# A fused attention and mixture-of-experts block: the slot's order rewritten with the projection in front, LayerNorms as a two-tensor operation, the last two weight centrings moved to VectorE

## The chip, the cores and the metric

The program runs on one NeuronCore of a Trainium2 chip. The core has TensorE (PE: matrix products and transposes into PSUM), VectorE (DVE), ScalarE (ACT) and GpSimd (POOL), each with its own instruction queue that is worked off strictly in order; SyncE (SP) issues transfers. The metric is the device time of one execution in microseconds, smaller is better. The kernel before took 807.15 us, the median of three runs (806.92 to 808.42).

## The reference

A sandwich block on x of shape 8 x 256 x 256 (batch, sequence, width), all float32. Attention has 16 query heads and 4 key/value heads of width 128; the expert layer has 8 experts of 176 hidden units, 2 for each token, and a shared expert of 352.

```
def layernorm(x): return (x - mean(x)) / sqrt(var(x) + 1e-5)          # over the last axis

# attention, on xn = layernorm(x)
q, k, v = split(xn @ w_qkv.T)                     # 16, 4 and 4 heads of 128
q = rope(layernorm(q) * qn_g + qn_b)              # rope(z) = z * cos + rotate_half(z) * sin
k = rope(layernorm(k) * kn_g + kn_b)
w = softmax(mask(q @ k.T / sqrt(128)))            # causal
x = x + layernorm((w @ v) @ w_o.T)

# experts, on xf = layernorm(x)
weights, indices = top_k(softmax(xf @ gate_w.T), 2); weights /= weights.sum()
out = sum over the chosen experts e of weights_e * ((silu(xf @ w_gate[e]) * (xf @ w_up[e])) @ w_down[e])
out += sigmoid(xf @ shgate_w) * ((silu(xf @ shw_gate) * (xf @ shw_up)) @ shw_down)
x = x + layernorm(out)
```

The mean of a head is taken out of the weights instead of the projected rows ("centring": the mean over the 128 columns of a head is subtracted from w_qkv), so that a head's LayerNorm needs only the mean of its squares.

## The kernel before

The kernel has two halves. The first runs attention for all eight batches and routes the tokens; the second runs the experts block by block. The change is in the first half, but for the LayerNorm helper, which both use.

**The slot loop.** After some hand-written steps at the start, the first half is one loop over slots s (L850). In each slot, functions issue one step each of several pipelines, and the order in which they stand in the loop body is the order on every engine's queue (`manual_schedule`: nothing is reordered). Twelve slots make a batch; there are 12 projections and 12 attention units in a batch. In slot s the loop works on projection j = s and on unit u = s - 7:

- `multiply(j)`, L384: the projection, four passes of 128x512 on PE into a PSUM tile `qkv`. Projection j is one group of 512 columns for one half of the sequence: k, k, v, v, then four pairs of q.
- `square`, L402, on ACT; `deviation`, L408, the sum of squares on DVE; `power`, L417, the reciprocal root on POOL. For v, `square` is only a copy (L399), and there is no LayerNorm or rope.
- `normalise`, L426: ACT scales the four heads from PSUM into `qn`.
- `rope_cos`, L440, on DVE and `rope_sin`, L452, two instructions on POOL, both read `qn`; `rope_offset`, L465, POOL, adds the table of offsets; `rope_sum`, L481, DVE, adds the two.
- `turn_heads`, L496: four transposes on PE into PSUM tile `tq`, and the copy to SBUF, L497, on ACT.
- `score`, L508 and L518 (PE); `maximum`, L528 (DVE); `exponential`, L539 (ACT); `inverse`, L547 (DVE); `weights`, on POOL (L554) for the units of four heads, every third unit, and on ACT (L559) for those of two; `turn_weights`, L570 (PE, PSUM tile `tp`); `copy_weights`, L575 (DVE); `value`, L588 (PE); `copy_value`, L599 (ACT); `output`, L607 (PE): the product with w_o of the batch before, 3, 3, 3, 3, 4, 0 steps in turn.

Some slots carry rarer steps. Counting slots within a batch as s mod 12: 0 and 6 have no output step and take the statistics of the finished attention rows (`residual`, then `residual_sum`); 1 and 7 those of the new residual (`inner`, `inner_rows`, which also writes the rows to memory by a transfer on SP's queue); 2 and 5 those of the next batch's x (`prepare`, `prepared`), transposed in 6 and 7 (`turn_x`). Slots 2 and 8 transpose the residual rows (`turn_inner`), 3 and 9 route (`route`, `gates`), 4 and 10 count and mark (`rank`, `mark`, `shares`), 5 and 11 enter the result (`enter`). All the row statistics have the same form: `norm_stats` (DVE L252, L253, L255; then POOL L256), `norm_apply` (DVE L261).

**Order within a slot.** normalise(j-1), rope_sum(j-2), turn_weights and copy_weights(u-2), copy_value(u-3), inverse and weights(u-1), score and maximum(u), rope_cos and rope_sin(j-1), then multiply(j), square(j), turn_heads(j-2), the statistics, `turn_x`, `turn_inner`, the routing, rope_offset(j-1), deviation(j) and power(j), the LayerNorms' second halves, exponential(u), output, value(u-2).

**Buffers.** PSUM has two tiles each for projections (`mm`), for transposes (`tr`, shared by tq, tp and the rarer ones) and for scores (`sc`), and one each for `av` and `o`.

**The start.** Of the six groups of w_qkv, group 4 is centred on DVE (`means`, `centre`), group 5 (v) not at all, and groups 0 to 3 have their means taken on DVE and the addition done in eight instructions each on ACT (`centre_on_act`, L242): groups 2 and 3 inside the loop, in slots 7 and 9. The x of batch 1 is prepared in slots 7 and 8 and transposed in 9 and 10 (`late_x`).

Of the kernel before, what the change touches and what calls it, by code (L numbers as in the profile page):

```python
# [19 lines left out]
P = 128  # L20
# [28 lines left out]
def block_kernel(  # L49
# [184 lines left out]
    def centre(heads, wm):  # L234
# [2 lines left out]
            in1=wm[:, :, None].to_broadcast([P, KC * REP, D]), op=ALU.add,  # L237
        )

    def centre_on_act(heads, wm):  # L240
        for i in range(KC * REP):
            nc.scalar.activation(  # L242
                heads[:, i, :], heads[:, i, :], AF.Identity, bias=wm[:, i : i + 1]
            )
# [13 lines left out]

    def norm_apply(dst, src, name):
        mean, rstd = stats.pop(name)  # L260
        nc.vector.tensor_scalar(dst, src, mean, rstd, ALU.subtract, ALU.mult)  # L261

    ps_mm = ctx.enter_context(tc.tile_pool(name="ps_mm", bufs=2, space=PSUM))
    ps_tr = ctx.enter_context(tc.tile_pool(name="ps_tr", bufs=2, space=PSUM))
# [73 lines left out]
    with ExitStack() as actx:  # L338
# [74 lines left out]
        def power(b, j):  # L413
            if projections[b][j][0] == 5:
                return
            rstd = small.tile([P, REP], F32, tag="rstds", name=f"rstds_{b}_{j}")
            nc.gpsimd.tensor_tensor(rstd, now.pop(("ve", b, j)), nhalf, ALU.pow)  # L417
            now["rstd", b, j] = rstd

        def normalise(b, j):  # L420
            if projections[b][j][0] == 5:
                return
            ps, rstd = now.pop(("mm", b, j)), now.pop(("rstd", b, j))
            qn = rw.tile([P, REP, D], F32, tag="qn", name=f"qn_{b}_{j}", bufs=2)
            for h in range(REP):
                nc.scalar.activation(  # L426
                    qn[:, h, :], ps[:, h, :], AF.Copy, scale=rstd[:, h : h + 1]
                )
            now["qn", b, j] = qn
# [53 lines left out]
        def turn_heads(b, j):  # L483
            g, t = projections[b][j]
            if g == 5:
                return
            if t == 0:
                if g == 4:
                    seqs[b]["kT"] = akv.tile([P, HKV, S], F32, tag="kT", name=f"kT_{b}")
                else:  # L490
                    seqs[b]["qT"][g] = q4pool.tile([P, REP, S], F32, tag="q4", name="q4")
            dst = seqs[b]["kT"] if g == 4 else seqs[b]["qT"][g]
            tr = ps_tr.tile([P, REP, P], F32, tag="tr", name=f"tq_{b}_{j}")
            t1 = now.pop(("t1", b, j))
            for h in range(REP):
                nc.tensor.transpose(tr[:, h, :], t1[:, h, :], ident)  # L496
            nc.scalar.copy(dst[:, :, t * P : (t + 1) * P], tr)  # L497
# [268 lines left out]
                if i == place and 0 < b < B - 1:  # L766
                    f(b + 1, t)

        late_x = {7: ([prepare], [prepared]), 8: ([prepare], [prepared]), 9: ([turn_x], []), 10: ([turn_x], [])}
        FIRST = LAG  # L770
        means_at = {8: 3}
        centre_at = {7: 2, 9: 3}
        found = {}
        with tc.manual_schedule():

# [45 lines left out]
            rope_sin(0, 4)  # L821
            deviation(0, 2)
            power(0, 2)
            centre_on_act(*found.pop(1))
            rope_sum(0, 1)
            turn_heads(0, 1)
            rope_sum(0, 4)
            turn_heads(0, 4)
            multiply(0, 3)
            multiply(0, 6)  # L830
            normalise(0, 2)
            square(0, 3)
            square(0, 5)
            rope_cos(0, 2)
            rope_offset_early(0, 2)
            rope_sin(0, 2)
            deviation(0, 5)
            power(0, 5)
            found[2] = means(2)
            normalise(0, 5)  # L840
            square(0, 6)
            rope_sum(0, 2)
            turn_heads(0, 2)
            rope_cos(0, 5)
# [1 line left out]
            rope_sin(0, 5)  # L846
            deviation(0, 6)
            power(0, 6)
            LAST = B * NS + LAG + 3
            for s in range(FIRST, LAST):  # L850
                u, j = s - LAG, s
                each(normalise, j - 1)
                each(rope_sum, j - 2)
                each(turn_weights, u - 2)
                each(copy_weights, u - 2)
                each(copy_value, u - 3)
                each(inverse, u - 1)
                each(weights, u - 1)
                each(score, u)
                each(maximum, u)  # L860
                each(rope_cos, j - 1)
                each(rope_sin, j - 1)
                if s == FIRST:
                    each(rope_offset_early, j - 1)
                each(multiply, j)
                each(square, j)
                each(turn_heads, j - 2)
                if s == B * NS + 1:
                    parked[0, 0] = products(0, 0)
                elif s == B * NS + 8:  # L870
                    parked[0, 1] = products(0, 1, ps_o, "o")
                ends(s, [(residual, 5), (inner, 6)])
                begins(s, [(prepare, 0, 2), (prepare, 1, 5), (turn_x, 0, 6), (turn_x, 1, 7)])
                if s in late_x:
                    for f in late_x[s][0]:
                        f(1, s - FIRST if f is prepare else s - FIRST - 2)
                ends(
                    s,
                    [(turn_inner, 7), (route, 8), (gates, 8), (rank, 9), (mark, 9), (shares, 9), (enter, 10)],
                )  # L880
                if s > FIRST:
                    each(rope_offset, j - 1)
                each(deviation, j)
                if s in means_at:
                    found[means_at[s]] = means(means_at[s])
                if s in centre_at:
                    centre_on_act(*found.pop(centre_at[s]))
                each(power, j)
                ends(s, [(residual_sum, 5), (inner_rows, 6)])
                begins(s, [(prepared, 0, 2), (prepared, 1, 5)])  # L890
                if s in late_x:
                    for f in late_x[s][1]:
                        f(1, s - FIRST)
                each(exponential, u)
                for b, i in [divmod(s - OUT, NS)]:
                    if 0 <= b < B:
                        for o in range(OUTPUTS[i]):
                            output(b, sum(OUTPUTS[:i]) + o)
                each(value, u - 2)
                if s == B * NS:  # L900

                    wgu_sb = wpool.tile([P, KC, E * 2 * HE], F32, tag="w", name="wgu_sb")
                    for j, w in enumerate((wg, wu)):
                        for c in range(KC):
                            nc.sync.dma_start(
                                out=wgu_sb[:, c, :].rearrange("p (e g h) -> p e g h", g=2, h=HE)[
                                    :, :, j, :
                                ],
                                in_=w[c * P : (c + 1) * P, : E * HE].rearrange(
                                    "p (e h) -> p e h", h=HE  # L910
                                ),
                            )
# [389 lines left out]
```

## Time and profile before

| | |
|---|---|
| median of three runs | 807.15 us |
| the profiled execution: time, span | 801.91 us, 799.9 us |
| PE busy | 742.7 us, 93% of the span |
| DVE busy | 553.4 us, 69% |
| POOL busy | 488.0 us, 61% |
| ACT busy | 443.5 us, 55% |
| granted TensorE clock | 0.992 of full speed |
| transfers | 32.40 MB, most of it in the first 20 us and the last 100 us |

The profiled execution took 2.0 us outside its span, and was 5.2 us faster than the median of the runs. Busy shares are means over the whole span. The loop's first batch runs from about 35 to 102 us; from there to about 567 us PE is busy nearly all the time, in a pattern that repeats every batch; the experts follow. A start time of the next instruction of the same queue minus that of an instruction says what it costs; its own duration is longer, since instructions overlap at their ends. Of PE's matrix products, four passes make one product of the projection, since float32 takes two passes and there are two chunks of the width.

### The profile page before, as it was taken

What the parts mean: (1) busy time and instruction counts of PE and PEld (TensorE: products, weight loads), DVE (VectorE), ACT (ScalarE), POOL (GpSimd) and SP (SyncE); (2) the same over time, 40 slices, a digit from 0 to 9 for tenths busy, and PEclk for the clock granted to TensorE, in tenths of its full rate; (3) what the DMA queues carried; (4) which work ended last, traced back from release to release, by engine and by line L of the source; (5) the groups of instructions that cost most, each with busy time, mean ns of one, the idle gap of its engine ahead of it and who ended that gap; (6) DMA issues with size and microseconds to landing.
All of it is one profiled execution on the core that took longest, in us unless ns stands there. A gap on an engine that the chain in (4) does not pass through costs nothing.

```text
span 799.9 us, 11918 instructions
## 1 busy us (share of the span) xinstructions
PE 742.7 (93%) x3765; PEld 550.3 (69%) x3796; DVE 553.4 (69%) x1396; ACT 443.5 (55%) x1426; POOL 488.0 (61%) x526
## 2 busy tenths in 40 slices
PE   7588899999999999999999999999799989999994
PEld 4355577767776676767677766777588767777773
DVE  7776666788777777877887777668755645354556
ACT  3587677665747575766657475756542323333331
POOL 5678588386848675774878486657611253656423
PEclk9899999999999999999999999999999999999998
DMA  9300000000000000000000000000400333434322
GB/s 314 123 0 1 1 0 2 7 7 2 8 1 7 1 7 1 8 0 8 8 1 8 1 7 1 7 1 8 144 8 9 85 93 99 139 101 131 106 86 79
DMA packets 26917, 32.40 MB, mean 41 GB/s; under 512 B 2980, under 2 KB 23048, under 8 KB 26856
## 3 DMA queue, kind: packets, MB, share of 16 engines
q1 hardware_dynamic: 22896, 22.07, 8.5%
q0 software_dynamic: 3408, 9.31, 4.5%
q8 instruction: 31, 0.51, 0.3%
q10 hardware_dynamic: 552, 0.26, 0.1%
q14 instruction: 30, 0.25, 0.1%
HBM read 22.33 MB, written 9.31 MB: 40 GB/s over the span
## 4 chain that ended last, share of the span: by engine, by line
PE 59%; POOL 14%; DVE 13%; ACT 10%; issue 2%; DMA 1%; POOLq 0%; DVEq 0%
PE qkv L384 11%; PE o L607 8%; PE sc L508 7%; PE gu L1128 6%; PE av L588 6%; ACT qn L426 6%; POOL rstds L417 5%; PE gus L279 5%; POOL t L452 5%; PE py L1153 4%; PE tp L570 3%; POOL t L465 3%; PE tq L496 3%; PE sd L299 2%; DVE ves L408 2%
## 5 line engine op out<-in xcount | busy, mean ns | idle before, releaser
L384 PE MATMUL qkv<-w_qkv,xnT 128*128 128x512 f32 x384 | 182.7, 598 | 1.3 <-DVE xnT L374 1.2
L426 ACT ACTIVATE qn<-qkv,rstds 128x128 f32<-128x128 f32 x320 | 91.5, 370 | 151.3 <-POOL rstds L417 151.3
L452 POOL TENSOR_TENSOR t<-qn,sg_q 128x256 f32<-128x256 f32 x128 | 123.7, 986 | 49.8 <-ACT qn L426 49.8
L417 POOL TENSOR_TENSOR rstds<-ves,nhalf 128x4 f32<-128x4 f32 x80 | 87.7, 1096 | 96.4 <-DVE ves L408 96.2
L607 PE MATMUL o<-wo_sb,oT 128*128 128x256 f32 x512 | 125.1, 384 | 0.0
L508 PE MATMUL sc<-kT,q 128*128 128x128 f32 x768 | 108.7, 275 | 4.0 <-ACT q L497 2.3
L539 ACT ACTIVATE ex<-sc,nmx 128x128 f32<-128x128 f32 (+1 forms) x256 | 107.8, 455 | 2.7 <-DVE nmx L528 2.4
L588 PE MATMUL av<-pT,v 128*128 128x256 f32 (+1 forms) x320 | 100.4, 428 | 8.0 <-ACT oT L599 7.3
L508 PEld LDWEIGHTS sc<-kT,q 128*128 128x128 f32 x768 | 100.8, 191 | 5.0 <-ACT q L497 3.0
L384 PEld LDWEIGHTS qkv<-w_qkv,xnT 128*128 128x128 f32 x384 | 66.1, 192 | 52.5 <-issue 46.7
L607 PEld LDWEIGHTS o<-wo_sb,oT 128*128 128x128 f32 x512 | 91.5, 190 | 9.4
L481 DVE TENSOR_TENSOR t<-t,t 128x512 f32<-128x512 f32 x80 | 55.2, 692 | 49.2 <-POOL t L465 49.2
L496 PEld LDWEIGHTS tq<-ident,t 128*128 128x128 f32 x320 | 38.6, 143 | 66.4 <-issue 54.0
L465 POOL TENSOR_TENSOR t<-t,bb_q 128x512 f32<-128x512 f32 x61 | 77.6, 1272 | 2.7
L575 DVE COPY pT<-tp 128x512 f32<-128x512 f32 x96 | 65.6, 683 | 18.2 <-PE tp L570 18.1
L559 ACT ACTIVATE ex<-ex,rr 128x256 f32<-128x256 f32 x128 | 59.6, 527 | 28.1 <-DVE rr L547 28.1
L588 PEld LDWEIGHTS av<-pT,v 128*128 128x128 f32 x320 | 58.5, 190 | 20.2 <-ACT oT L599 10.5
L570 PEld LDWEIGHTS tp<-ident,ex 128*128 128x128 f32 x384 | 47.1, 141 | 31.5 <-ACT q L497 9.9
L496 PE MATMUL tq<-ident,t 128*128 128x128 f32 x320 | 49.4, 279 | 20.3 <-DVE t L481 20.3
L528 DVE TENSOR_REDUCE nmx<-sc 128x2 f32<-128x512 f32 (+1 forms) x96 | 64.2, 669 | 3.8 <-PE sc L508 3.4
L440 DVE TENSOR_TENSOR t<-qn,cg_q 128x512 f32<-128x512 f32 x64 | 47.5, 742 | 26.7 <-ACT qn L426 26.7
L408 DVE TENSOR_REDUCE ves<-sq 128x4 f32<-128x516 f32 x80 | 54.8, 685 | 14.2 <-ACT sq L402 14.2
(185 smaller groups left out, 1302.5 us busy)
## 6 DMA issues: line engine op xcount, KB each, us to landing
ys<-yb SPq DMA_DIRECT2D x39, 128.0 KB, 1.8
w_qkv<-in_wqkvT SPq DMA_DIRECT2D x6, 512.0 KB, 6.0
x_all<-in_x SPq DMA_DIRECT2D x8, 256.0 KB, 7.2
wo_sb<-in_woT SPq DMA_DIRECT2D x1, 2048.0 KB
xf_rows<-xf SPq DMA_DIRECT2D x16, 128.0 KB, 1.7
out<-yo SPq DMA_DIRECT2D x16, 128.0 KB, 1.7
wgu_sb<-in_wg SPq DMA_DIRECT2D x2, 704.0 KB, 5.3
wgu_sb<-in_wu SPq DMA_DIRECT2D x2, 704.0 KB, 8.4
```

The lines of the kernel that those rows point to most:

```text
L384: nc.tensor.matmul(ps.rearrange("p h d -> p (h d)"), lhsT=seqs[b]["xnT"][t][:, c, :], rhs=w_qkv[g][:, c, :], start=(c == 0), stop=(c == KC ...
L408: nc.vector.tensor_reduce(out=ve, in_=now.pop(("sq", b, j))[:, :, : D + 1], axis=AX.X, op=ALU.add)
L417: nc.gpsimd.tensor_tensor(rstd, now.pop(("ve", b, j)), nhalf, ALU.pow)
L426: nc.scalar.activation(qn[:, h, :], ps[:, h, :], AF.Copy, scale=rstd[:, h : h + 1])
L452: nc.gpsimd.tensor_tensor(t2[:, :, lo : lo + HD], qn[:, :, hi : hi + HD], sg[s][:, t : t + 1, lo : lo + HD].to_broadcast([P, REP, HD]), AL ...
L465: nc.gpsimd.tensor_tensor(t2, t2, bb[s][:, t : t + 1, :].to_broadcast([P, REP, D]), ALU.add)
L496: nc.tensor.transpose(tr[:, h, :], t1[:, h, :], ident)
L508: nc.tensor.matmul(sc[:, h, k * P : (k + 1) * P], lhsT=seqs[b]["qT"][g][:, r0 + h, t * P : (t + 1) * P], rhs=seqs[b]["kT"][:, g, k * P : ( ...
L539: nc.scalar.activation(ex[:, h, :], sc[:, h, :], AF.Exp, bias=nm[:, h : h + 1], accum_out=rs[:, h : h + 1],)
L570: nc.tensor.transpose(tr[:, c, :], ex[:, h, k * P : (k + 1) * P], ident)
L588: nc.tensor.matmul(now["av"][:, r0 : r0 + nh, :].rearrange("p h q -> p (h q)"), lhsT=seqs[b]["v"][:, k, g * D : (g + 1) * D], rhs=pT[:, k ...
L607: nc.tensor.matmul(now["o", b, t], lhsT=seqs[b]["oT"][h // REP, t][:, h % REP, :], rhs=wo_sb[:, h, :], start=(h == 0), stop=(h == H - 1),)
```

## The change

Five things change.

1. **The order within a slot.** `multiply(j)` goes to the front. Then follow normalise(j-1), rope_sum(j-2), inverse(u-1), copy_value(u-3), rope_cos(j-1), square(j), weights(u-1), rope_sin(j-1), turn_weights and copy_weights(u-2), deviation(j) and power(j), score and maximum(u), turn_heads(j-2), the statistics, rope_offset(j-1), the LayerNorms' second halves, exponential(u), output, `turn_x`, `turn_inner` and the routing, value(u-2). On POOL, power(j) and the statistics' powers so stand ahead of rope_offset(j-1); on DVE, copy_weights stands behind the cosine product, deviation between it and maximum, and the routing at the end of the slot.
2. **LayerNorms on rows.** `norm_apply` is a `scalar_tensor_tensor`, whose second tensor is the reciprocal root, repeated along the row, where it was a `tensor_scalar` with two scalars per partition.
3. **Centring.** Group 2 is centred on DVE ahead of the loop; group 3 on DVE in two halves, in slots 7 and 8 (`centre_chunk`). None is left to ACT inside the loop.
4. **The x of batch 1** is prepared in slots 9 and 10 and transposed in 11 and 12.
5. **The steps ahead of the loop** are put in another order: among others projection 6 ahead of projection 3, and square(5), deviation(5) and power(5) earlier.

```diff
+    def centre_chunk(g, c):
+
+        heads = w_qkv[g][:, c, :].rearrange("p (h d) -> p h d", d=D)
+        wm = small.tile([P, REP], F32, tag="wmc", name=f"wm_{g}_{c}")
+        nc.vector.tensor_reduce(out=wm, in_=heads, axis=AX.X, op=ALU.add)
+        nc.vector.tensor_scalar_mul(wm, wm, -1.0 / D)
+        nc.vector.tensor_tensor(
+            out=heads, in0=heads, in1=wm[:, :, None].to_broadcast([P, REP, D]), op=ALU.add
+        )
...
     def norm_apply(dst, src, name):
         mean, rstd = stats.pop(name)
-        nc.vector.tensor_scalar(dst, src, mean, rstd, ALU.subtract, ALU.mult)
+        nc.vector.scalar_tensor_tensor(
+            dst, src, mean, rstd.to_broadcast([P, HID]), ALU.subtract, ALU.mult
+        )
...
-        late_x = {7: ([prepare], [prepared]), 8: ([prepare], [prepared]), 9: ([turn_x], []), 10: ([turn_x], [])}
+        late_x = {9: ([prepare], [prepared]), 10: ([prepare], [prepared]), 11: ([turn_x], []), 12: ([turn_x], [])}
         FIRST = LAG
-        means_at = {8: 3}
-        centre_at = {7: 2, 9: 3}
         found = {}
...
             power(0, 2)
+            square(0, 5)
             centre_on_act(*found.pop(1))
             rope_sum(0, 1)
             turn_heads(0, 1)
             rope_sum(0, 4)
             turn_heads(0, 4)
+            normalise(0, 2)
+            multiply(0, 6)
             multiply(0, 3)
-            multiply(0, 6)
-            normalise(0, 2)
-            square(0, 3)
-            square(0, 5)
+            deviation(0, 5)
+            power(0, 5)
             rope_cos(0, 2)
             rope_offset_early(0, 2)
             rope_sin(0, 2)
-            deviation(0, 5)
-            power(0, 5)
-            found[2] = means(2)
             normalise(0, 5)
             square(0, 6)
+            square(0, 3)
             rope_sum(0, 2)
...
             power(0, 6)
+            centre(*means(2))
             LAST = B * NS + LAG + 3
             for s in range(FIRST, LAST):
                 u, j = s - LAG, s
+                each(multiply, j)
                 each(normalise, j - 1)
                 each(rope_sum, j - 2)
-                each(turn_weights, u - 2)
-                each(copy_weights, u - 2)
+                each(inverse, u - 1)
                 each(copy_value, u - 3)
-                each(inverse, u - 1)
+                each(rope_cos, j - 1)
+                each(square, j)
                 each(weights, u - 1)
-                each(score, u)
-                each(maximum, u)
-                each(rope_cos, j - 1)
                 each(rope_sin, j - 1)
                 if s == FIRST:
                     each(rope_offset_early, j - 1)
-                each(multiply, j)
-                each(square, j)
+                each(turn_weights, u - 2)
+                each(copy_weights, u - 2)
+                each(deviation, j)
+                each(power, j)
+                each(score, u)
+                each(maximum, u)
                 each(turn_heads, j - 2)
...
                 ends(s, [(residual, 5), (inner, 6)])
-                begins(s, [(prepare, 0, 2), (prepare, 1, 5), (turn_x, 0, 6), (turn_x, 1, 7)])
-                if s in late_x:
-                    for f in late_x[s][0]:
-                        f(1, s - FIRST if f is prepare else s - FIRST - 2)
-                ends(
-                    s,
-                    [(turn_inner, 7), (route, 8), (gates, 8), (rank, 9), (mark, 9), (shares, 9), (enter, 10)],
-                )
+                begins(s, [(prepare, 0, 2), (prepare, 1, 5)])
+                if s in late_x and prepare in late_x[s][0]:
+                    prepare(1, s - 9)
                 if s > FIRST:
                     each(rope_offset, j - 1)
-                each(deviation, j)
-                if s in means_at:
-                    found[means_at[s]] = means(means_at[s])
-                if s in centre_at:
-                    centre_on_act(*found.pop(centre_at[s]))
-                each(power, j)
                 ends(s, [(residual_sum, 5), (inner_rows, 6)])
                 begins(s, [(prepared, 0, 2), (prepared, 1, 5)])
                 if s in late_x:
                     for f in late_x[s][1]:
-                        f(1, s - FIRST)
+                        f(1, s - 9)
+                if s in (FIRST, FIRST + 1):
+                    centre_chunk(3, s - FIRST)
                 each(exponential, u)
                 for b, i in [divmod(s - OUT, NS)]:
                     if 0 <= b < B:
                         for o in range(OUTPUTS[i]):
                             output(b, sum(OUTPUTS[:i]) + o)
+                begins(s, [(turn_x, 0, 6), (turn_x, 1, 7)])
+                if s in late_x and turn_x in late_x[s][0]:
+                    turn_x(1, s - 11)
+                ends(s, [(turn_inner, 7), (route, 8), (gates, 8), (rank, 9), (mark, 9), (shares, 9), (enter, 10)])
                 each(value, u - 2)
```

## The prediction, made before the changed kernel was run

> **What bounds the kernel now.** I read the busy shares, then busy time by stretches, then the list of waits, then PE's and the side engines' timelines. Over one batch in the middle:
>
> ```profile
> 350.59:423.88 73.29, 70.99 (x374) 52.18 (x377) 57.26 (x140) 46.55 (x154) 50.93 (x53) 1.00 0.01 5
> ```
>
> (columns: stretch, length, then PE, weight loads, DVE, ACT, POOL; clock, DMA.) PE is at its limit, 70.99 of 73.29 us; no other engine is over 78%. The list of waits opens with an entry that looks like the thing to remove:
>
> ```profile
> ACT qn L426 <- POOL rstds L417: 151.3, 77, 3.6
> ```
>
> ACT waits 151 us for the power, but ACT has slack; it costs only what reaches PE. PE's timeline says how much that is:
>
> ```profile
> 345.50 0.63 PE L496 MATMUL tq<-ident,t 128*128 128x128 f32 x4 [0.95 <-DVE t L481]
> 353.44 1.12 PE L588 MATMUL av<-pT,v 128*128 128x512 f32 x2 [0.53 <-ACT oT L599]
> 390.25 0.65 PE L570 MATMUL tp<-ident,ex 128*128 128x128 f32 x4 [0.64 <-ACT q L497]
> ```
>
> A head transpose, a value product and a weight transpose wait once in a batch each. From start-to-start times (a transpose group costs 0.44, not its 0.60) the losses are 1.11, 0.69 and 0.81: 2.6 us a batch, about six batches, so 16 us is all that the steady part can give. The first batch (35.18 to 102.39 us, no outputs) loses more: 56.15 busy of 67.4 us.
>
> **What sets the pace beside PE** is the contention of DVE and POOL:
>
> ```profile
> 322.50 0.55 POOL L256 TENSOR_TENSOR rstd_f<-mv_f,nhalf 128x1 f32<-128x1 f32 x1
> 323.02 1.27 POOL L465 TENSOR_TENSOR t<-t,bb_q 128x512 f32<-128x512 f32 x1
> 323.09 1.36 DVE L261 TENSOR_SCALAR xf<-x_all,mv_f,rstd_f 128x256 f32<-128x256 f32 x1
> ```
>
> The row LayerNorm starts 0.07 us behind POOL's rope offset and ends 0.16 after it; alone it takes 0.41. A DVE operation with two SBUF tensors is held too:
>
> ```profile
> 575.96 0.72 POOL L622 TENSOR_TENSOR x_all<-x_all,y 128x256 f32<-128x256 f32 x1
> 576.03 1.19 DVE L481 TENSOR_TENSOR t<-t,t 128x512 f32<-128x512 f32 x1 [0.69 <-POOL t L465]
> ```
>
> That rope sum normally takes 0.69.
>
> **What the Trainium skill says.** "SBUF — State Buffer", section "SBUF: two separate sides": DVE and GpSimd share one port pair, held exclusively for a whole instruction by a GpSimd operation, by a DVE operation in a two-port mode, and, against a GpSimd operation that reads SBUF, by a DVE operation with two SBUF inputs. The lines above agree. "VectorE: DVE Perf Modes", section "The perf-mode tier table": float32 from SBUF, tensor_scalar runs at twice tensor_tensor's rate. Here the only scalar_tensor_tensor of 128x256 (L1174, L1178) takes 0.48 against 0.41.
>
> **The change, part by part.** A slot's work on PE is the same, in another cycle; its durations (start to start): projection 1.72, tp 0.44, scores 1.01, tq 0.44, 0.43 per output step, value 0.86, rarer steps 0.2 to 0.4. So a slot takes 4.5 to 4.7 without outputs (0 and 6), 5.8 to 6.1 with three, 6.65 with four.
>
> *Removed: the wait of normalise.* Power(j) now follows deviation(j) in mid-slot, before normalise(j) is due. So oT and q are copied in time, and their two waits (0.69, 0.81) lose that cause.
>
> *Added: a chain through the rope sum.* tq(j-2) needs rope_sum(j-2), which needs rope_offset(j-2); this now stands on POOL behind power(j-1) and the statistics' power of the slot before, and these wait for DVE's variance, maximum and statistics. On DVE the order is sum, reciprocal, cosine, copy, variance, maximum, statistics. From one rope sum to the next, with the start-to-start times of the rows: 0.61 + 0.07 + 0.61 + 0.60 + 0.62 + 0.66 + 0.82 (three statistics instructions) + 0.09 handing over + 0.51 power + 1.27 offset + 0.04 = 5.90 us. Before, normalise, rope_sin, offset and power closed the chain, but the sum was 1.1 us ahead of its transpose (318.42 + 0.69 against 320.25). Queued behind a late sum on DVE stand the reciprocal (POOL's or ACT's weights wait for it), the cosine, copy_weights (the value product) and the variance (the next power), so a late sum is late for all of them.
>
> Slot by slot, against PE's own need:
> - 6 to 7: after the offset POOL goes straight on to the residual addition (L622, y is ready by then), so the sum takes 1.19 as above: 5.90 + 0.50 = 6.4. PE could do it in 4.7; before it took 5.81. Less 0.1 of slack at slot 6: +0.5.
> - 0 to 1: the same, 6.4, less 0.55 slack, since slot 11 is the longest: 5.85, before 5.35: +0.5.
> - 7 to 8 and 1 to 2: the LayerNorm behind the offset holds DVE 0.3 more: 6.2, against PE's 6.05 and 5.83: +0.15 and +0.37.
> - 8 to 9 and 11 to 0: POOL's weights come first: sum, reciprocal and cosine 1.4, weights 1.0, sin 1.4, power 1.0, offset 1.3 = 6.1, against 6.03 and 6.65: +0.06.
> - 9 to 10: no statistics, 5.0: 0. Slots 3 to 5 have little rope: 0.
> - 10 to 11: rank and mark, 2.65 us unhindered plus about 1.1 held by the offset, still stand ahead of the sum: stall 1.0, was 1.11: 0.
>
> In slots 6 and 0 copy_weights, now 1.3 us later on DVE, delays the value product by 0.3 to 0.6; the figures of 6.4 cover that. Sum: +1.6 us a batch, six batches: **+9.5**.
>
> *The LayerNorm operation.* Of its 32 uses from SBUF in the first half 24 are held now, for 1.36, and I expect them to stay held: with two SBUF tensors the instruction asks for the same port. I take 0.34 behind the offset's end (a held 512-wide tensor_tensor ends 0.55 after, less 0.21 for half the width) for 0.15 before; bounds: -0.9 each, if it slips through, to +0.3. The 16 that read PSUM were never held (0.54) and stay. The 16 at the end cost 0.07 each, one on the last path: **+0.1**. What it hides behind in the loop is in the sums above.
>
> *The start.* Eight ACT instructions (2.45 us) leave slots 7 and 9 each, where the projection waited for them (3.6 us in all); DVE gets 2.6 us (1.21 + 0.17 + 1.22) ahead of rope_sum(5), which delays tq(5) by about 1.1, and 1.4 in slots 7 and 8 each. Followed row by row, tq(7) comes at 48.6 instead of 49.69, tq(10) at 66.95 instead of 66.75, tq(16) at 96.3 instead of 97.19, and the first output slot about 1.9 earlier: **-2**, bounds -5 to +2.
>
> *Moved with it.* The transfer of xf is issued at the same place of its slot; SP's queue has nothing else until the expert weights (after the last projection), 0.32 us: 0. turn_x and the routing go ahead of value; tx waits for xn of slots earlier, and route for a copy of the slot before: 0. `gates` (ACT) now stands ahead of the next normalise and waits for DVE's routing: normalise(9) about 1.8 late, absorbed because DVE is on rank next; without that cover up to 0.7 a batch.
>
> Sum: 9.5 + 0.1 - 2 = +7.6 on the profiled 801.91, so 809.5; on the median, whose runs were 5.2 slower, **814.7**.
>
> **Rivals.**
> *(A) Faster.* The slack gathered in slots 3 to 5 and 11 covers the new chain, all three PE waits go, and the opening gains 3: 6 x 2.6 + 3 = 18.6, 788.5; half of it, 798. For it: DVE and POOL average 78% and 69%. Against: the chain has DVE and POOL in series, and 0 and 6 are a third shorter on PE than the chain. It decides if the chain is below 5.3 us.
> *(B) Slower by more.* Where `qn` is ready before the offset ends, POOL goes on to rope_sin and takes the port ahead of the sum and the cosine: 0.6 more in some four slots without POOL weights, 2.4 a batch, +14 on top: 829. For it: ACT's exponentials end at about 4.3 and normalise at 5.4 of a 5.9 chain. Against: in the trace the waiting engine gets the port next (at 62.67 the sin's first half takes 1.18 for its usual 0.73, while a waiting cosine goes).
> *(C) No difference.* Gains and losses of 2.6 against 1.6 plus the rest cancel: 806 to 808.5.
> *(D) The LayerNorm does what it is worded for* and is not held: 24 held rows give back 0.9, two of the slots above lose their +0.15 and +0.37: 3 us less, inside the forecast.
>
> **How the numbers follow.** Forecast 0.40 (own range 809 to 822), B 0.13, A 0.36, C 0.11. Below 0.2% (1.6 us) this kernel's runs can't tell a change. So faster 0.36, same 0.11, slower 0.53. A's upper half and B's lower half give the range, 794 to 829.
>
> **What would show it.** Right: qn's wait for rstds nearly gone; tq's wait for the rope sum grown from 1 us to 3 or more a batch, at slots 7, 1 and 11; rope sums after the residual addition at 1.19; row LayerNorms from SBUF near 1.5; batch period near 74.9. Wrong: a period of 71 with PE waits under 1 us a batch, or LayerNorm rows at 0.48 in the loop.

## The result and the profile after

The changed kernel takes **832.73 us** (median, 831.13 to 832.9) beside 807.78 us (806.92 to 809.87) for the kernel before in the same comparison (runs of the kernels taken together on one chip): ratio **1.0306**, 95% interval 1.0287 to 1.0325, so slower by about 25 us. The forecast was 814.7, its range ended at 829.

The second half of the program (the experts) took 124.5 to 125.3 us from its first to its last gate-and-up product in some executions and 128.9 to 134.3 in others, for kernels with either loop, so spans can differ by 5 us or more without the change having a part in it; times are therefore compared as ratios within a comparison, and profiles by marks inside the first half. The profile of before (799.9 us, 124.5 in that part) was of the first sort, that of after (830.9, 130.1) of the second: of the 31.0 us between the two spans 25.3 lie ahead of the last output product (620.44 against 645.77). Nearly all of the other 5.7 lie in the expert half; the repetition below shows why they aren't put down to the change.

The page of the changed kernel, busy time of the engines and the chain that ended last (before, the chain was 59% PE, 14% POOL, 13% DVE and 10% ACT):

```profile
PE 752.1 (91%) x3796; PEld 558.5 (67%) x3796; DVE 579.8 (70%) x1401; ACT 450.2 (54%) x1410; POOL 481.2 (58%) x526
...
DVE 38%; PE 34%; POOL 20%; issue 3%; ACT 2%; DMA 1%; POOLq 0%; SPq 0%; DVEq 0%; ACTq 0%
```

DVE and POOL took the chain over from PE. One batch in the middle, from a head transpose to the same one ten later (columns: stretch, length, then PE, weight loads, DVE, ACT, POOL; clock, DMA):

```profile
373.37:449.93 76.56, 71.46 (x376) 52.76 (x377) 59.75 (x141) 48.23 (x155) 50.00 (x53) 1.00 0.01 4
```

The batch is 76.55 us long where it was 73.28: +3.27 (forecast +1.6). PE's own work has hardly moved (71.46 against 70.98 over such a batch of before); DVE is busy for 59.75 where it was 57.25, of which its LayerNorm rows explain 0.4 (59.34 without them, e1 below). The list of waits:

```profile
POOL rstds L429 <- DVE ves L420: 114.4, 50, 8.6
...
DVE t L493 <- POOL t L477: 58.6, 37, 2.7
...
PE tq L508 <- DVE rr L559: 20.6, 36, 3.0
...
PE tq L508 <- DVE t L493: 15.7, 10, 6.1
...
ACT qn L438 <- POOL rstds L429: 12.6, 24, 2.3
...
PE av L600 <- DVE pT L587: 9.8, 12, 1.2
```

The wait that the change takes away is gone (qn for rstds 151.3, now 12.6). In its place PE's head transposes wait for DVE's rope sum, 3.2 us in a steady batch where it was 0.9 (the reciprocal `rr` stands right behind the sum, so the list names it in most of the cases; the transposes don't read it), and value products wait for DVE's copy of the weights. Where DVE's time went is seen in its timeline, here slot 0 of a batch:

```profile
363.90 1.26 POOL L477 TENSOR_TENSOR t<-t,bb_q 128x512 f32<-128x512 f32 x1
...
365.17 1.86 POOL L464 TENSOR_TENSOR t<-qn,sg_q 128x256 f32<-128x256 f32 x2
365.19 1.26 DVE L493 TENSOR_TENSOR t<-t,t 128x512 f32<-128x512 f32 x1 [1.97 <-POOL t L477]
...
366.37 0.15 DVE L559 RECIPROCAL rr<-rs 128x2 f32<-128x2 f32 x1
366.45 1.14 DVE L452 TENSOR_TENSOR t<-qn,cg_q 128x512 f32<-128x512 f32 x1
```

The rope offset (L477) ends at 365.16. The sine (L464) is next in POOL's queue and has its qn already; it starts 0.01 later. The rope sum (L493) is released by the same end and starts 0.02 behind the sine, held: 1.26 for its usual 0.69. The sine's second half then holds the cosine (L452) to 1.14 for its 0.66. In slot 1 a residual addition (L634) stands on POOL between the offset and the sine:

```profile
371.95 0.73 POOL L634 TENSOR_TENSOR x_all<-x_all,y 128x256 f32<-128x256 f32 x1
372.02 1.20 DVE L493 TENSOR_TENSOR t<-t,t 128x512 f32<-128x512 f32 x1 [0.76 <-POOL t L477]
372.64 2.31 POOL L464 TENSOR_TENSOR t<-qn,sg_k 128x256 f32<-128x256 f32 x2
373.15 0.15 DVE L559 RECIPROCAL rr<-rs 128x2 f32<-128x2 f32 x1
373.22 1.14 DVE L452 TENSOR_TENSOR t<-qn,cg_k 128x512 f32<-128x512 f32 x1
```

Here the addition holds the sum and the sine the cosine. Over the kernel 39 sums of 80 take 1.0 or more (1 of 80 before), 26 of them held by the sine and 13 by the addition, and 43 cosines of 80 are above 1.1 (2 before). The means of the groups of sums and q cosines, which were 692 and 742 ns before:

```profile
L493 DVE TENSOR_TENSOR t<-t,t 128x512 f32<-128x512 f32 x80 | 74.7, 935 | 59.2 <-POOL t L477 58.6
...
L452 DVE TENSOR_TENSOR t<-qn,cg_q 128x512 f32<-128x512 f32 x64 | 60.2, 940 | 5.1 <-ACT qn L438 5.0
```

In a steady batch the sine holds the sum in slots 6, 9 and 0 (0.34, 0.56, 0.57 us) and the cosine in slots 6, 7, 9, 0 and 1 (0.48 each): 3.9 us in all. (In slot 6 DVE comes to the sum late, when the sine has run for 0.44.) That was one of the rivals, and the theory to be tested.

In the kernel before, the next instruction on POOL behind the offset was not the sine but the power, for 74 of 75 offsets, and a power doesn't hold the sum:

```profile
317.11 1.27 POOL L465 TENSOR_TENSOR t<-t,bb_q 128x512 f32<-128x512 f32 x1
318.35 1.02 POOL L417 TENSOR_TENSOR rstds<-ves,nhalf 128x4 f32<-128x4 f32 x1
318.42 0.69 DVE L481 TENSOR_TENSOR t<-t,t 128x512 f32<-128x512 f32 x1 [0.69 <-POOL t L465]
...
320.62 1.92 POOL L452 TENSOR_TENSOR t<-qn,sg_q 128x256 f32<-128x256 f32 x2 [0.56 <-ACT qn L426]
```

There 57 sums of 80 begin and end inside a power of 1.0 to 1.4 us and take 0.68 to 0.69. The change moved the power ahead of the offset, and so left the sine next behind it.

### The profile page after: what moved, and what is told of

Its sections match the earlier page's. It is cut to its first block, busy times and chain, and to the rows that moved or that the text cites. A ratio compares the mean times of both kernels' runs of the same rounds, so it can differ in the third digit from the quotient of the medians.

```text
span 830.9 us, 11948 instructions
## 1 busy us (share of the span) xinstructions
PE 752.1 (91%) x3796; PEld 558.5 (67%) x3796; DVE 579.8 (70%) x1401; ACT 450.2 (54%) x1410; POOL 481.2 (58%) x526
## 4 chain that ended last, share of the span: by engine, by line
DVE 38%; PE 34%; POOL 20%; issue 3%; ACT 2%; DMA 1%; POOLq 0%; SPq 0%; DVEq 0%; ACTq 0%
DVE t L493 7%; DVE t L452 6%; PE gu L1135 6%; POOL t L477 5%; PE o L619 5%; PE gus L291 5%; POOL t L464 4%; POOL rstds L429 4%; PE py L1160 4%; POOL ex L566 4%; DVE ves L420 4%; DVE pT L587 3%; PE qkv L396 3%; DVE nmx L540 3%; PE av L600 2%
## 5 line engine op out<-in xcount | busy, mean ns | idle before, releaser
L551 ACT ACTIVATE ex<-sc,nmx 128x128 f32<-128x128 f32 (+1 forms) x256 | 104.7, 417 | 105.8 <-DVE nmx L540 105.6
L429 POOL TENSOR_TENSOR rstds<-ves,nhalf 128x4 f32<-128x4 f32 x80 | 81.5, 1019 | 114.5 <-DVE ves L420 114.4
L464 POOL TENSOR_TENSOR t<-qn,sg_q 128x256 f32<-128x256 f32 x128 | 114.8, 916 | 12.7 <-ACT qn L438 12.5
L396 PEld LDWEIGHTS qkv<-w_qkv,xnT 128*128 128x128 f32 x384 | 73.5, 194 | 69.8 <-issue 62.6
L493 DVE TENSOR_TENSOR t<-t,t 128x512 f32<-128x512 f32 x80 | 74.7, 935 | 59.2 <-POOL t L477 58.6
L600 PE MATMUL av<-pT,v 128*128 128x256 f32 (+1 forms) x320 | 103.3, 437 | 10.5 <-DVE pT L587 9.8
L438 ACT ACTIVATE qn<-qkv,rstds 128x128 f32<-128x128 f32 x320 | 91.3, 378 | 12.6 <-POOL rstds L429 12.6
L566 POOL TENSOR_TENSOR ex<-ex,rr 128x512 f32<-128x512 f32 x32 | 41.6, 1301 | 72.6 <-DVE rr L559 71.7
L477 POOL TENSOR_TENSOR t<-t,bb_q 128x512 f32<-128x512 f32 x61 | 77.7, 1274 | 0.0
L508 PEld LDWEIGHTS tq<-ident,t 128*128 128x128 f32 x320 | 36.2, 144 | 45.6 <-DVE t L493 13.7
L600 PEld LDWEIGHTS av<-pT,v 128*128 128x128 f32 x320 | 53.8, 191 | 18.8 <-ACT q L509 8.3
L452 DVE TENSOR_TENSOR t<-qn,cg_q 128x512 f32<-128x512 f32 x64 | 60.2, 940 | 5.1 <-ACT qn L438 5.0
```

Of the source, the lines that this page charges most:

```text
L396: nc.tensor.matmul(ps.rearrange("p h d -> p (h d)"), lhsT=seqs[b]["xnT"][t][:, c, :], rhs=w_qkv[g][:, c, :], start=(c == 0), stop=(c == KC ...
L438: nc.scalar.activation(qn[:, h, :], ps[:, h, :], AF.Copy, scale=rstd[:, h : h + 1])
L452: nc.vector.tensor_mul(t1, now["qn", b, j], cg[s][:, t : t + 1, :].to_broadcast([P, REP, D]))
L464: nc.gpsimd.tensor_tensor(t2[:, :, lo : lo + HD], qn[:, :, hi : hi + HD], sg[s][:, t : t + 1, lo : lo + HD].to_broadcast([P, REP, HD]), AL ...
L477: nc.gpsimd.tensor_tensor(t2, t2, bb[s][:, t : t + 1, :].to_broadcast([P, REP, D]), ALU.add)
L493: nc.vector.tensor_add(t1, t1, now.pop(("t2", b, j)))
```

## The experiments

Each ratio is to the kernel before in the same comparison. "Batch" is the steady distance of ten head transposes in the experiment's profile. The loads at the start come earlier or later from one execution to the next: the second projection begins at 11.0 to 11.6 us, in e1 at 12.0 and in e10 at 14.1. So the last column counts the first output from the start of the second projection, and openings are compared by that.

| kernel | ratio | 95% interval | batch, us | first output, us | from 2nd projection, us |
|---|---|---|---|---|---|
| before | 1 | | 73.28 | 104.77 | 93.74 |
| changed | 1.0306 | 1.0287 to 1.0325 | 76.55 | 108.70 | 97.55 |
| e5_changed_again | 1.0282 | 1.0260 to 1.0304 | 76.61 | 109.04 | 97.58 |
| e1_rows_ts | 1.0280 | 1.0262 to 1.0297 | 76.17 | 109.18 | 97.15 |
| e2_old_opening | 1.0322 | 1.0305 to 1.0340 | 76.58 | 110.33 | 99.11 |
| e3_old_loop | 1.0036 | 1.0022 to 1.0049 | 73.75 | 105.72 | 94.17 |
| e4_sin_behind_sum | 0.9982 | 0.9972 to 0.9991 | 72.93 | 104.26 | 93.12 |
| e7_before_sin_behind | 0.9990 | 0.9978 to 1.0002 | 73.34 | 104.75 | 93.53 |
| e8_cos_later | 1.0215 | 1.0177 to 1.0254 | 75.56 | 108.22 | 96.79 |
| e9_cos_later_act | 1.0231 | 1.0210 to 1.0252 | 75.53 | 106.47 | 95.13 |
| e6_sin_behind_ts | 0.9939 | 0.9918 to 0.9961 | 72.53 | 103.65 | 92.63 |
| e10_residual_later | 0.9919 | 0.9901 to 0.9936 | 72.57 | 106.70 | 92.60 |

**Which part of the change costs?** Three kernels undo one part each. The first:

```diff
-        nc.vector.scalar_tensor_tensor(
-            dst, src, mean, rstd.to_broadcast([P, HID]), ALU.subtract, ALU.mult
-        )
+        nc.vector.tensor_scalar(dst, src, mean, rstd, ALU.subtract, ALU.mult)
```

> The changed kernel with one part undone: the LayerNorm on rows is a tensor_scalar again. My theory (the 25 us are lost in the loop, between the rope sum, the rope sine and the port): the row operation is held behind POOL's offset in either form, for 1.48 us now and about 1.36 then, so at most 0.13 us in each of some 24 rows, less 16 PSUM rows that become 0.06 longer: 830 to 833, and the 76.5 us batch stays within 0.3. Rival (the two-tensor form takes the port from POOL and is the cause): the batch falls to about 74 to 75 and the time to 815 to 822. The expert half, which is 5.7 us longer in the changed kernel (170.8 against 165.1 from the table of experts to the end) and for which I have no cause: if the two-tensor form is that, 165 here and 827.

The batch falls by 0.38, the rows from SBUF are held still (1.3 to 1.4 in 26 of 32), and the intervals of the two ratios overlap. The LayerNorm is worth some 2 us of the 25. It isn't what makes the expert half long: that took 125.0 here, and 125.3 in e4 below, which has the new form.

The second takes the opening of the kernel before with the new loop: its list of steps ahead of the loop, `late_x` at slots 7 to 10, and in the loop

```diff
-                if s in (FIRST, FIRST + 1):
-                    centre_chunk(3, s - FIRST)
+                if s in means_at:
+                    found[means_at[s]] = means(means_at[s])
+                if s in centre_at:
+                    centre_on_act(*found.pop(centre_at[s]))
```

> The changed kernel with another part undone: the opening of the kernel before (its order ahead of the loop, centring on ACT in slots 7 and 9, the second sequence's LayerNorm at slots 7 and 8), with the new loop and the new LayerNorm. By the marks of the two profiles the first output came 3.9 us later after the change (108.70 against 104.77), where I had forecast 2 earlier. Theory 1: the new loop order loses it, in slots 9 to 12 and 16 to 18, and the new opening itself is worth about the 2 us of my forecast: without it the time is about 835. Theory 2: the new opening (centring on DVE ahead of rope sums) costs the 4 us: 829, first output near 105. The steady batch stays at 76.5 in both.

The first theory: counted from the second projection, the first output comes 1.5 to 1.6 later with the old opening, not earlier. The ratios of the two overlap, so the gain is read from the marks alone, and it belongs to this loop: in the old one (next kernel) the new opening, with the new LayerNorm, has its first output 0.4 later than before.

The third keeps opening and LayerNorm and puts the loop's order back (projection in mid-slot behind the sine, power behind the offset):

```diff
             for s in range(FIRST, LAST):
-                each(multiply, j)
                 each(normalise, j - 1)
                 each(rope_sum, j - 2)
...
                 each(rope_sin, j - 1)
...
+                each(multiply, j)
+                each(square, j)
...
                     each(rope_offset, j - 1)
+                each(deviation, j)
+                each(power, j)
```

> The kernel before with the new opening and the new LayerNorm operation only, so the changed kernel with the loop's order undone. Theory: the loop's order is worth the +3.27 us of each of six batches, so the batch is back at 73.2 to 73.5 and the time at about 808 plus or minus what the opening does: 806 if the opening gains 2 as I forecast, 811 to 812 if it loses 4. Rival (the LayerNorm's new form makes the batches long): batch above 74.5, time above 815.

1.0036 is 806.5 us beside 803.2: 22 of the 25 us are the loop's order. The batch keeps +0.47; of the two parts left, the opening has no step in a steady batch, so this is the LayerNorm's form in this order.

**What of the loop's order?** One size is changed, the number of buffers of the sine's tile, so that a slot's sine can't start before the sum of the slot before has read its own (the four tiles that are written ahead of the loop lie in a buffer of the softmax's tiles):

```diff
-            t2 = rw.tile([P, REP, D], F32, tag="t2", name=f"t2_{b}_{j}", bufs=2)
+            if b == 0 and j < 6:
+                t2 = sw.tile([P, REP, D], F32, tag="ex", name=f"t2_{b}_{j}")
+            else:
+                t2 = rw.tile([P, REP, D], F32, tag="t2", name=f"t2_{b}_{j}", bufs=1)
```

> The changed kernel with one size changed: the tile of the rope sine has one buffer in the loop instead of two (the five early ones lie in a buffer of the softmax tiles), so a slot's sine cannot start before the rope sum of the slot before has read its tile. Theory (the sine takes the port ahead of the sum): the sums that are held by the sine (some 28 of 80, 0.5 us each) run in 0.69 again; about 13 behind the residual addition stay at 1.2. If the cosine is not then held in the sum's place, the time falls by 5 to 14 us, to 819 to 828. Rival 1 (the hold only moves: the sine now starts in the reciprocal and holds the cosine, so 40 or more cosines at 1.14): 830 to 834, batch 76 to 77. Rival 2 (POOL becomes the chain: sine, power and offset start later by the sum's time): above 836.

It is more than I expected: the whole loss is gone, and the kernel is level with the one before or a little ahead. Its timeline, slot 0 again:

```profile
421.65 1.26 POOL L480 TENSOR_TENSOR t<-t,bb_q 128x512 f32<-128x512 f32 x1
...
422.95 0.69 DVE L496 TENSOR_TENSOR t<-t,t 128x512 f32<-128x512 f32 x1 [1.97 <-POOL t L480]
...
423.56 0.16 DVE L562 RECIPROCAL rr<-rs 128x2 f32<-128x2 f32 x1
423.63 0.67 DVE L452 TENSOR_TENSOR t<-qn,cg_q 128x512 f32<-128x512 f32 x1
423.79 1.80 POOL L467 TENSOR_TENSOR t<-qn,sg_q 128x256 f32<-128x256 f32 x2 [0.87 <-DVE rr L562]
```

The sum runs in 0.69; the cosine begins 0.16 ahead of the sine and runs in 0.67, and now the sine is the one that is held (1.80 for 1.41). That costs nothing here: the power behind it on POOL waits for DVE's variance anyhow, and in this slot starts 0.08 us after its end in both kernels. The batch:

```profile
430.10:503.03 72.93, 71.14 (x376) 52.93 (x377) 56.03 (x141) 48.31 (x155) 48.69 (x53) 1.00 0.01 5
```

DVE is down from 59.75 to 56.03, by 3.7 us, and the batch by 3.62: nearly all of the hold had reached PE. The sums behind the residual addition stay at 1.20, and cosines above 1.1 are 5. Per slot, the distance from one head transpose to the next (medians of five steady batches; slots 4 and 5 have no head transpose):

| slots | before | changed | e4 | forecast of the change | changed | e4 less before |
|---|---|---|---|---|---|---|
| 6 to 7 | 5.80 | 6.64 | 5.83 | +0.50 | +0.84 | +0.03 |
| 7 to 8 | 5.97 | 6.74 | 6.27 | +0.15 | +0.77 | +0.30 |
| 8 to 9 | 5.97 | 6.44 | 6.00 | +0.06 | +0.47 | +0.03 |
| 9 to 10 | 6.30 | 6.33 | 6.30 | 0 | +0.03 | 0 |
| 10 to 11 | 6.97 | 6.73 | 6.37 | 0 | -0.24 | -0.60 |
| 11 to 0 | 6.81 | 6.69 | 6.69 | 0 | -0.12 | -0.12 |
| 0 to 1 | 5.35 | 6.61 | 5.58 | +0.50 | +1.26 | +0.23 |
| 1 to 2 | 5.80 | 6.42 | 5.94 | +0.37 | +0.62 | +0.14 |
| 2 to 3 | 6.18 | 6.00 | 6.00 | 0 | -0.18 | -0.18 |
| 3 to 6 | 18.12 | 17.95 | 17.95 | 0 | -0.17 | -0.17 |

From changed to e4, 6 to 7 falls by 0.81, which is the hold on the sum and the cosine of slot 6 (0.34 + 0.48), and 0 to 1 by 1.03 (0.57 + 0.48).

**Is the one buffer a gain of its own?** The same edit on the kernel before:

> The kernel before with only the one buffer for the sine's tile. Theory: there the sine already waits for its qn, which comes late (behind the power), so that only 1 of 80 sums and 2 of 80 cosines run at 1.2: the sine is never ahead of the sum and nothing changes: ratio 0.998 to 1.003. Rival (one buffer is a gain of its own in any order, by spacing POOL's and DVE's work): 0.99 or less.

Nothing, as expected: the sine was behind the sum already. So the edit acts through the sine's place alone. The reason that I gave, the late qn, is only one of two: by the lines of before above, the power alone ends 0.26 us after the sum, so the sine would have come behind the sum with its qn ready too.

**Sum or cosine?** The sine is left free and the cosine is put behind copy_weights.

```diff
-                each(rope_cos, j - 1)
                 each(square, j)
                 each(weights, u - 1)
                 each(rope_sin, j - 1)
...
                 each(copy_weights, u - 2)
+                each(rope_cos, j - 1)
```

> The changed kernel with the sine free to go ahead of the sum as there (two buffers), but the cosine placed on DVE behind copy_weights, that is 0.6 us later, when the sine is over. It takes the hold off the cosine and leaves it on the sum. Theory (both holds are on the chain: 28 sums by 0.5 and 40 cosines by 0.46, 14 and 18 us of DVE, of which 26 reached the time): sums as before at about 1.2, cosines at 0.69, and rather more than half of the loss gone, ratio 1.01 to 1.015. Rival 1 (only the sum's hold counts, because the sum alone releases PE): 1.028 to 1.031. Rival 2 (only the cosine's counts): 1.00.

This miss was of my design: the cosine got out of the sine's way and into POOL's weights (27 times held, 21 of them to 1.2 or more), so the gain of 1 us a batch tells nothing of the question. The next kernel does it only where ACT computes the weights:

```diff
+                later = u >= 2 and shape((u - 1) % NS)[0] != REP
+                if not later:
+                    each(rope_cos, j - 1)
...
                 each(copy_weights, u - 2)
+                if later:
+                    each(rope_cos, j - 1)
```

> The changed kernel, two buffers and the sine free, with the cosine behind copy_weights only in the slots whose softmax weights are ACT's, where the sine follows the offset directly; where POOL computes the weights, the cosine stays. The try before moved it everywhere, and there it ran into POOL's weights instead (28 times at 1.2), so it told nothing. By the changed kernel's rows the sine's first half holds the sum in slots 6, 9 and 0 (0.34, 0.56, 0.57 us) and its second half the cosine in slots 6, 7, 9, 0 and 1 (0.48 each): 1.47 and 2.4 us a batch, 3.9 together, of which 3.6 came back with the sine behind the sum. Theory (both lie on the same chain and simply add): cosines at 0.69, the sums stay held, 2.0 to 2.4 us of the batch come back: 74.1 to 74.5, ratio 1.010 to 1.015. Rival 1 (only the sum counts, since only the sum releases PE): batch 76.3 or more, ratio 1.026 or more. Rival 2 (only the cosine counts): batch about 73, ratio 1.00.

As a total it missed (75.53 for 74.1 to 74.5): the cosine is free only in slots 6, 9 and 0. In slots 7 and 1 the sine starts behind the residual addition and is still running when the moved cosine comes (1.24), and in slot 10 the cosine now meets a late sine (1.21 for 0.69). By slot it answers the question. Slot 0 of a batch (the sum held, the cosine free):

```profile
434.69 1.26 POOL L477 TENSOR_TENSOR t<-t,bb_q 128x512 f32<-128x512 f32 x1
...
435.97 1.87 POOL L464 TENSOR_TENSOR t<-qn,sg_q 128x256 f32<-128x256 f32 x2
435.99 1.26 DVE L493 TENSOR_TENSOR t<-t,t 128x512 f32<-128x512 f32 x1 [1.96 <-POOL t L477]
...
437.83 0.68 DVE L452 TENSOR_TENSOR t<-qn,cg_q 128x512 f32<-128x512 f32 x1
```

(this form is the same in slots 6, 9 and 0). The distance 6 to 7 goes from 6.64 to 6.16 and 0 to 1 from 6.61 to 6.13: 0.48 each, the whole of the cosine's hold, with the sum's left. Both holds count, and they add.

**A repetition of the changed kernel**, for the expert half:

> The changed kernel itself, unaltered, beside the others. In its first profile the expert half, which the loop's order doesn't touch, was 5.5 us longer than before (130.1 against 124.5 from the first to the last gate-and-up product), while in the four experiments so far it was 124.8 to 125.3. Theory: that was that execution's, not the change's: 125 here, a span some 5 us shorter, batch again 76.5. Rival: the combination of new opening and new LayerNorm does it (each of the experiments but one lacked one of them or shifted the phase): 130 again.

The ratio is that of the first comparison within the intervals, the batch is the same. The expert half was 131.5 us again, against my expectation; but e7, which has the old loop, old opening and old LayerNorm, had 131.5 in the same comparison, and the four kernels of the comparison with e1 to e4 had 124.8 to 125.3. So it goes with the comparison and not with the kernel (the three comparisons of the experiments ran on three chips); the kernel before itself took 803.2, 807.2 and 810.2 us in them. Why some need 5 us more there was not tried.

**Can both be beaten?** The sine behind the sum and the row LayerNorm as it was:

> The changed kernel with the sine behind the sum and the LayerNorm on rows as a tensor_scalar again. Theory: the gains add, since the rows' longer hold (1.48 against 1.36) stands in front of two sums of a batch: the batch falls from 72.93 by 0.3 to 0.5 (76.54 to 76.17 without the sine's order, 73.75 against 73.28 in the old loop), 2 to 3 us in all: ratio to the kernel before about 0.995. Rival: with the sum no longer late the rows stand off the path, and nothing is gained: 0.998.

The gains add: 0.9939, batch 72.53. The last kernel, built on that, takes the residual addition from behind the offset. The step that is moved, `residual_sum`, holds a LayerNorm on DVE as well (0.54), which now stands between the cosine and copy_weights:

```diff
                 each(rope_sin, j - 1)
+                ends(s, [(residual_sum, 6)])
...
-                ends(s, [(residual_sum, 5), (inner_rows, 6)])
+                ends(s, [(inner_rows, 6)])
```

> The version with the sine behind the sum and the tensor_scalar rows, and in addition the residual addition on POOL moved from behind the offset to behind the sine of the next slot. In slots 7 and 1 the sum behind it was held to 1.20. Theory (any POOL instruction that is ready behind the offset takes the port ahead of the sum; the residual addition is the other one): these sums run in 0.69, and 0.3 to 0.5 us come back in each of two slots, since the addition now lies where POOL waits for the variance: batch from 72.53 to 71.6 to 72.0, ratio to the kernel before 0.986 to 0.990. Rival (it delays the power and so the next offset by its own 0.72): batch 72.4 to 73, ratio 0.994 to 1.000.

Its slot 1, where the sum stood at 1.20:

```profile
428.42 1.27 POOL L478 TENSOR_TENSOR t<-t,bb_q 128x512 f32<-128x512 f32 x1
...
429.73 0.69 DVE L494 TENSOR_TENSOR t<-t,t 128x512 f32<-128x512 f32 x1 [1.90 <-POOL t L478]
...
432.32 0.72 POOL L635 TENSOR_TENSOR x_all<-x_all,y 128x256 f32<-128x256 f32 x1
```

The theory on the port is right for the addition: 78 sums of 80 are at 0.7. Its "any POOL instruction" goes too far, as the power in the kernel before shows. On the time the rival is right. The distance 6 to 7 falls from 5.70 to 5.19 and 7 to 8 grows from 6.13 to 6.67: the power now comes behind the addition, and its variance behind the LayerNorm, so the next offset is late by what was saved. Batch 72.57, ratio within e6's interval; the first output at 106.70 is the late start of this one execution, and not the edit's. Both e6 and e10 are faster than the kernel before, by 0.6 and 0.8 in 100 with intervals that end below 1, and so faster than the changed one.

## Why the prediction was wrong, step by step

*Normalise's wait.* Right: 151.3 to 12.6 us. PE's waits of the value product for oT and of the weight transpose for q are gone from the steady batch.

*The chain of 5.90 from sum to sum.* Right in size where no port hold is in it: in e4 the steps from sum to sum are 5.79 from slot 6 to 7 and 5.80 from 0 to 1. In the changed kernel they are 6.60 and 6.83.

*What PE pays for it, +1.6 a batch.* Wrong: without the sine's hold (e4, which has the new order but for the sine's place) the batch is 0.35 shorter than before. The five slots for which I forecast +1.58 give +0.73. In 6 to 7 and 0 to 1 I had 0.1 and 0.55 us of slack for the 0.5 of the residual addition; the table gives +0.03 and +0.23. The slack was larger: in e4 the sums of slots 6 and 0 end 0.63 and 0.87 ahead of their transposes, where transposes that wait for their sum (slots 7 and 1) start 0.15 behind it, so 0.48 and 0.72. And I set the rest to 0 where it gains 1.07, of which 0.60 in 10 to 11, the rank slot: I had taken over its stall of 1.0 unchanged. So my largest term, +9.5, had the wrong sign.

*Rival B was what happened*, and I gave it 13 in 100. Its mechanism and place (the sine directly behind the offset, in slots without POOL weights) were right. That its 829 lies within 4 us of the 832.73 is in part luck: I had 2.4 a batch from the sine on top of 1.6 from the chain, 4.0; it is 3.62 on top of -0.35, 3.27; and the start, which I had as a gain, made up the difference. The failing step is the argument against it, that "the waiting engine gets the port next". The example was a cosine that had begun ahead of the sine. The sum is not waiting at the port when the offset ends: it waits for the offset, and POOL's own next instruction starts at that moment. In slots 9 and 0 the sine starts 0.01 us behind the offset's end and the sum 0.03, and the sum runs 1.26 for 0.69. The condition that I named ("where qn is ready before the offset ends") was met by the change itself, in two ways: it takes away normalise's wait (in slot 0 qn is done 0.07 before the offset's end), and it takes the power, inside which the sum had run unheld, from between the offset and the sine.

*A sign that came true for another reason.* I had said that the transposes' wait for the sum would grow from 1 us to 3 or more a batch if the forecast is right. It is 3.2; without the sine's hold (e4) it is 1.7. So this sign couldn't tell the forecast from rival B; the batch of 76.55 for 74.9 could.

*The LayerNorm.* Held in the loop, 1.48 in 26 rows (forecast about 1.5, an end 0.34 behind the offset's; it is 0.28). Its PSUM rows are shorter, 0.48 for 0.54. It costs about 0.4 a batch on PE (76.55 to 76.17, 73.28 to 73.75, 72.93 to 72.53), some 2.5 in all; I had that in slots 7 to 8 and 1 to 2, and it shows in 6 to 7 too (6.64 against 6.50 in e1). Rival D is out. From the last gate-and-up product to the end 28.31 to 28.33 with the new form and 28.17 to 28.18 with the old: +0.14 for +0.1.

*The start.* The new opening alone gains 1.5 to 1.6 at the first output in the new loop (e2 beside the changed kernel), near my -2. But counted from the second projection the first output came 3.8 later than before, because the sine holds sums and cosines in the first batch too: with it behind the sum (e4) it comes 0.6 earlier than before. The step that failed is the same one, and without it my -2 would still have been too much.

*The sum.* At the last output product: +3.9 at the first output, six times about 3.3, and the end of the last batch are the 25.3; the forecast's +7.6 lacked the sine.

## What to carry to other kernels

When a change takes away a wait or moves an instruction, ask what these had been keeping in order: here the power behind the offset, and ACT's late normalise, kept POOL's sine behind DVE's sum, and nobody had written that order down. Where two engines share a port, list for each release who is ready at that moment; in these traces the engine that produced the value went on with its next instruction at once (0.01 us), and the consumer on the other engine came second (0.03). An order that matters can be made explicit with a buffer count (e4: one buffer fewer was worth 3 in 100).

## What the runs showed of the hardware

- A DVE rope sum (two SBUF operands) that starts 0.02 us behind the first half of POOL's sine, or 0.08 behind a residual addition, ends 0.55 after that instruction: 1.26 and 1.20 for 0.69. The other way round, POOL's sine with a cosine begun 0.16 ahead takes 1.80 for 1.41. "SBUF — State Buffer", section "SBUF: two separate sides", of the Trainium skill says that whichever of the two starts first has the pair for its whole instruction, and for these instructions the trace agrees. What I had not expected is who starts first: the POOL instruction queued behind the one that releases the sum, 0.01 against 0.03 us after that one's end (the residual addition even 0.04 before it).
- For POOL's power (128x4, 1.0 to 1.4 us) the trace does not agree with that sentence: in the kernel before, 57 sums run wholly inside one, begun 0.07 us or more behind its start, and take 0.68 to 0.69. Why this operation holds nobody was not tried. So what stands behind the offset decides: a power costs the sum nothing, a sine or an addition over half a microsecond.
- A hold moves rather than ends. The sine's 3.9 us of DVE a batch went away only where the held side had slack (POOL in e4). A cosine moved by 0.6 us ran into POOL's weights (e8), and a residual addition moved by half a slot, with its LayerNorm, delayed the power by as much as it had held the sum (e10).
